# Constants packed on the host and loaded in few transfers, the attention's beside the filter's network, and that network on two chunks at once

## The chip, the core and the metric

The kernel runs on one core of one Trainium2 chip. A core has five engines that run side by side, each through its own instruction stream in order: TensorE (PE) for matmuls, VectorE (DVE), ScalarE (ACT), GpSimd (POOL) and SyncE (SP). In this kernel SP issues all transfers between DRAM and the on-chip memory; the transfers themselves are done by 16 DMA engines. The metric is the device time of one run, in microseconds (us), taken as the median of several runs. The time before is 12442.48 us, the median of 3 runs from 12437.2 to 12442.61.

## What is computed

The input x is [32, 192, 56, 56] in f32. Four layers follow each other, each with a group normalisation in front (32 groups) and a residual sum:

```python
x = x + _L0_conv_ref(_gn(x), ...)   # agent attention: qkv, 49 pooled agents, 6 heads, 3x3 depthwise, projection
x = x + _L1_conv_ref(_gn(x), ...)   # two-way WKV scan over 3136 tokens, layer norm, output projection
x = x + _L2_conv_ref(_gn(x), ...)   # shift by rounded offsets, then a 3x3 Gaussian of the remainder
x = x + _L3_conv_ref(_gn(x), ...)   # long convolution with a generated 55x55 filter, by FFT
```

The filter of the last layer comes from a small network over the 55 x 55 = 3025 positions:

```python
h = jnp.sin(f1 * (jnp.einsum('bchw,oc->bohw', z, W1) + b1))     # 32 -> 64
h = jnp.sin(f2 * (jnp.einsum('bchw,oc->bohw', h, W2) + b2))     # 64 -> 64
k = jnp.einsum('bchw,oc->bohw', h, W3)                          # 64 -> 192
k = k * (jnp.exp(-distance_map * jnp.abs(deltas)) + shift)
```

Its Fourier spectrum doesn't depend on the images and is needed only in the last layer.

## The kernel before

`all_blocks` (L1813) calls four parts one after the other: `make_filter` (L201), `attention` (L321), `scan_pairs` (L898, with a guarded second version that is entered only if a count is above zero) and `channel_blocks` (L1509). Between the parts the images go through DRAM (`x1`, `x2`). The parts are written in a framework in which each engine's order comes from a scheduler, and waits are put in where a tile's data or its memory demand it. A part's tiles come from pools that are opened in the part; the pools of the next part take over the same memory, and what is written there first waits for what used it last.

**The filter.** SP loads 12 constants (helper L212, issued at L214). The network (loop of 11 chunks of 275 positions, before `loaded`) does for each chunk: matmul with W1 (L261), a sine (`sine`, L243), matmul with W2 (L264), a second sine, a copy into `h2_i` (L267). A sine is seven DVE instructions (L246 to L253: scale, range reduction, clamp) and one of ACT (L255). W1's and W2's outputs are 64 rows, so these instructions work on 64 of 128 partitions. Chunk i's second sine and chunk i+1's first run interleaved. Then for each half t of the 192 channels the decay (ACT, L275) and, chunk by chunk, the product with W3 (PE, L278) times decay (DVE, L280); half t is stored to `filt` (SP, L285). The products of t = 0 are spread over the network's loop by the scheduler; those of t = 1 follow it. The second stage reads `filt` back in six batches of 32 channels (L301), makes spectra by two matmuls each with copies on ACT and DVE (L1801, L1807, L311, L314) and stores them to `spectra`.

**The attention.** Before its first image SP issues 128 transfers for constants: weights of q, k and v in forms for 128 and 64 or 65 rows (L348), the projection's blocks (`_Pairs.blocks`, L860 to L864), vectors (L870, L872), matrices for norms and heads (L348), four pieces of an interpolation matrix into rows 64 to 124 of `xs_c` (61 rows each, L397), and two tables of bias coefficients, `gk_c` and `gq_c`, in 96 small transfers (L407 to L410). Then images 0 and 1 are loaded (`load`, L445). For an image: statistics (`moments`, L452: L457 and L459 BatchNorm statistics, L461/L462, row sums L466, pooled sums L469 to L477), group sums on PE (L487), scale and offset (L504 to L509), pooled agents (L520), keys of the agents (L532, L533, `seen`), normalised image pieces `xs_a` and `xs_c` (L544, L548), values (`find_v`, L563 to L576), depthwise taps (L589, L591), and then the loop over images that begins with `weigh` (L596; matmuls L604, L605). Inside the loop the next image is loaded and its statistics are taken beside the current one's matmuls.

**The scan's start.** 52 constant transfers: two halves each of Wo, the layer norm's gain and bias and a centring matrix, 24 blocks and more for Wk, Wv, Wr, the output matrix, centring, mean and group (`blocks`), and two vectors in three pieces each. The output matrix `wog` is Wo times the gain, centred; it is made by L941 to L951, written to DRAM (`wogT`, L952) and read back in six blocks. Behind them SP loads the sums of squares (`seen`, L1053) that the attention has left in DRAM; from these come group means on PE (L1016 and on), and the first normalisation is ACT's L1100. The decay and bonus vectors pass through L963 to L980 first.

**The channel blocks' start.** Nine constants (L1530), eight whole memsets of `padded` on POOL (L1539), then the offsets (`off`, L1544) and a chain of small DVE instructions (L1545 to L1572) that makes the taps' weights; POOL makes the shift matrices (L1586 to L1591) and PE starts with L1594.

Of the kernel before, what the change touches and what calls it, by code (L numbers as in the profile page):

```python
# [29 lines left out]
T = 96  # L30
# [44 lines left out]

def _constants():
# [16 lines left out]
    for t in range(2):  # L93
# [4 lines left out]
    heads = np.kron(np.eye(2), np.ones((AG, HD)))  # L98
    return {
        "spread": spread,  # L100
        "norm4": norm4.reshape(128, 4, 128),
        "ident": np.eye(128),
        "group": group,
        "center": center,
        "group192": np.kron(np.eye(C // GROUP), np.ones((GROUP, GROUP))) / GROUP,
        "centre": np.eye(C) - 1.0 / C,
        "mean192": np.full((C, C), 1.0 / C),
        "mean": np.full((T, T), 1.0 / C),
        "heads": heads,
        **_spectral_constants(),  # L110
# [90 lines left out]
def make_filter(ctx: ExitStack, tc: tile.TileContext, a, consts, filt, spectra):  # L201
# [3 lines left out]
    wp = ctx.enter_context(tc.tile_pool(name="f_w", bufs=2))  # L205
    pp = ctx.enter_context(tc.tile_pool(name="f_p", bufs=2, space=PSUM))
# [5 lines left out]
    def load(name, shape, ap):  # L212
# [5 lines left out]
    w2 = load("w2", [FO, FO], a["L3_conv_W2T"])  # L218
    w3 = load("w3", [FO, C], a["L3_conv_W3T"])
    z = load("z", [FE, P2], a["L3_conv_z"].rearrange("b c h w -> (b c) (h w)"))  # L220
    bs = [load(k, [FO, 1], a[f"L3_conv_{k}"].unsqueeze(1)) for k in ("b1", "b2")]
    fs = [
        load(k, [FO, 1], a[f"L3_conv_{k}"].rearrange("a c h w -> c (a h w)"))
        for k in ("f1", "f2")
    ]
    per = {}
    for k in ("deltas", "shift", "bias"):
        per[k] = load(
            k, [T, 2], a[f"L3_conv_{k}"].rearrange("a (t p) h w -> p (a t h w)", p=T)
        )  # L230
    dist = load(
        "dist", [T, P2], a["L3_conv_distance_map"].rearrange("a b h w -> (a b h w)").partition_broadcast(T)
    )
    nd = cp.tile([T, 2], F32, name="nd", tag="nd")
# [8 lines left out]
    def sine(ps, b, f):  # L243

        v = wp.tile([FO, n], F32, name="v", tag="v")
        nc.vector.tensor_scalar(v, ps, b, f, ALU.add, ALU.mult)  # L246
        m = wp.tile([FO, n], F32, name="m", tag="m")
        nc.vector.tensor_scalar(m, v, 1.0 / (2.0 * math.pi), None, ALU.mult)
        nc.vector.tensor_scalar(m, m, BIG, None, ALU.add)
        nc.vector.tensor_scalar(m, m, BIG, None, ALU.subtract)  # L250
        nc.vector.scalar_tensor_tensor(v, m, -C1, v, ALU.mult, ALU.add)
        nc.vector.scalar_tensor_tensor(v, m, -C2, v, ALU.mult, ALU.add)
        nc.vector.tensor_scalar(v, v, EDGE, -EDGE, ALU.min, ALU.max)  # L253
        h = wp.tile([FO, n], F32, name="h", tag="h")
        last = nc.scalar.activation(h, v, AF.Sin)  # L255
        return h, last

    sines = []
    for i in range(KS // RC):
        p1 = pp.tile([FO, BANK], F32, name="p1", tag="p1")  # L260
        nc.tensor.matmul(p1[:, :n], w1, z[:, i * n : (i + 1) * n], start=True, stop=True)  # L261
        h1, _ = sine(p1[:, :n], bs[0], fs[0])
        p2 = pp.tile([FO, BANK], F32, name="p2", tag="p1")
        nc.tensor.matmul(p2[:, :n], w2, h1, start=True, stop=True)  # L264
        h2, last = sine(p2[:, :n], bs[1], fs[1])
        keep = cp.tile([FO, n], F32, name=f"h2_{i}", tag=f"h2_{i}")
        nc.vector.tensor_copy(keep, h2)  # L267
        sines.append(keep)
# [4 lines left out]
    for t in range(2):  # L273
        decay = wp.tile([T, P2], F32, name="decay", tag="decay")
        nc.scalar.activation(decay, dist, AF.Exp, scale=nd[:, t : t + 1])  # L275
        for i in range(KS // RC):
            p3 = pp.tile([T, BANK], F32, name="p3", tag="p3")
            nc.tensor.matmul(p3[:, :n], w3[:, t * T : (t + 1) * T], sines[i], start=True, stop=True)  # L278
# [40 lines left out]

@with_exitstack  # L320
def attention(ctx: ExitStack, tc: tile.TileContext, a, k, x1, st_a, st_c):  # L321
# [11 lines left out]
    xp = ctx.enter_context(tc.tile_pool(name="a_x", bufs=2))  # L333
# [11 lines left out]
    def const(name, shape, *parts):  # L345
        t = cp.tile(shape, F32, name=name, tag=name)
        for to, ap in parts:
            nc.sync.dma_start(out=to(t), in_=ap)  # L348
        return t

    def all_of(t):
        return t

    pairs = _Pairs(nc, cp)
    qkv, qkvb = a["L0_conv_Wqkv"], a["L0_conv_bqkv"]

    def taking(name, col):

        return (
            const(f"{name}_a", [128, C], (all_of, qkv[0:128, col : col + C])),  # L360
            const(
                f"{name}_c",
                [65, C],
                (lambda t: t[0:64], qkv[128:C, col : col + C]),
                (lambda t: t[64:65], qkvb[col : col + C].unsqueeze(0)),
            ),
        )

    def giving(name, row):

        w = a["L0_conv_WqkvT"]
        return (
            const(f"{name}_a", [128, C + 1], (all_of, w[row : row + 128])),
            const(f"{name}_c", [64, C + 1], (all_of, w[row + 128 : row + C])),
        )

    wq, wv = taking("wq", 0), taking("wv", 2 * C)
    wqT, wkT = giving("wqT", 0), giving("wkT", C)
    proj = pairs.blocks("proj", a["L0_conv_proj_w"])
    pb, dwb = pairs.vector("pb", a["L0_conv_proj_b"]), pairs.vector("dwb", a["L0_conv_dwc_b"])  # L380
    dw = a["L0_conv_dwc_w"].rearrange("p o h w -> p (o h w)")
    dww = const(
        "dww",
        [128, 2, 9],
        (lambda t: t[:, 0, :], dw[0:128]),
        (lambda t: t[UP, 1, :], dw[128:C]),
        (lambda t: t[LOW, 1, :], dw[128:C]),
    )
    ident = const("ident", [128, 128], (all_of, k["ident"]))
    norm4 = const("norm4", [128, 4, 128], (all_of, k["norm4"]))  # L390
    heads = const("heads", [PAIR, 2 * HD], (all_of, k["heads"]))
# [3 lines left out]
    xs_c = [cp.tile([128, S * w], F32, name=f"xs_c{j}", tag=f"xs_c{j}") for j, w in enumerate(WIDTHS)]  # L395
    for j, w in enumerate(WIDTHS):
        nc.sync.dma_start(out=xs_c[j][64:KC], in_=k["spread"][:, S * STARTS[j] : S * (STARTS[j] + w)])  # L397

    def coefficients(name, grid, cols, rows):

        t = cp.tile([128, 2 * NK, HA], F32, name=name, tag=name)
        nc.gpsimd.memset(t, 0.0)
        g = grid.rearrange("(y x) c -> y x c", x=POOL)
        for j, w in enumerate(WIDTHS):
            for h in range(2):
                y0, x0 = 3 * h, GRID[j]
                nc.sync.dma_start(out=t[65:93, 2 * j + h], in_=rows[28 * h : 28 * h + 28])  # L407
                nc.sync.dma_start(out=t[93 : 93 + w, 2 * j + h], in_=cols[STARTS[j] : STARTS[j] + w])
                for y in range(4):
                    nc.sync.dma_start(out=t[109 + 4 * y : 113 + 4 * y, 2 * j + h], in_=g[y0 + y, x0 : x0 + 4])  # L410
        return t

    gk_c = coefficients("gk_c", a["anT"], a["awT"], a["ahT"])
    gq_c = coefficients("gq_c", a["naT"], a["waT"], a["haT"])
# [29 lines left out]

    def load(b):  # L445
        x = xp.tile([128, S, S], F32, name="x_a", tag="x_a"), xp.tile([128, S // 2, S], F32, name="x_c", tag="x_c")
        nc.sync.dma_start(out=x[0], in_=a["x"][b, 0:128])
        for h, r in HALVES:
            nc.sync.dma_start(out=x[1][r], in_=a["x"][b, 128:C, 28 * h : 28 * h + 28])
        return x  # L450
# [318 lines left out]
    nxt = load(0)  # L769
# [8 lines left out]
    for b in range(NB):  # L778
        x, more = nxt, b + 1 < NB
        if more:  # L780
            nxt = load(b + 1)
# [58 lines left out]
class _Pairs:  # L840
# [3 lines left out]
    def __init__(self, nc, pool):  # L844
        self.nc, self.pool = nc, pool

    def blocks(self, name, ap, inner=True):

        nc = self.nc
        aa = self.pool.tile([128, 128], F32, name=f"{name}_aa", tag=f"{name}_aa")  # L850
        ca = self.pool.tile([128, 128], F32, name=f"{name}_ca", tag=f"{name}_ca")
        if not inner:
            nc.sync.dma_start(out=aa, in_=ap[0:128, 0:128])
            for r in (slice(0, 64), slice(64, 128)):
                nc.sync.dma_start(out=ca[r], in_=ap[128:C, 0:128])
            return aa, ca, None, None
        ac = self.pool.tile([128, 64], F32, name=f"{name}_ac", tag=f"{name}_ac")
        cc = self.pool.tile([128, 128], F32, name=f"{name}_cc", tag=f"{name}_cc")
        nc.gpsimd.memset(cc, 0.0)  # L859
        nc.sync.dma_start(out=aa, in_=ap[0:128, 0:128])  # L860
        nc.sync.dma_start(out=ac, in_=ap[0:128, 128:C])
        for r in (slice(0, 64), slice(64, 128)):
            nc.sync.dma_start(out=ca[r], in_=ap[128:C, 0:128])
            nc.sync.dma_start(out=cc[r, r], in_=ap[128:C, 128:C])  # L864
        return aa, ca, ac, cc

    def vector(self, name, ap):

        t = self.pool.tile([128, 2], F32, name=name, tag=name)
        self.nc.sync.dma_start(out=t[:, 0:1], in_=ap[0:128].unsqueeze(1))  # L870
        for r in (slice(0, 64), slice(64, 128)):
# [1009 lines left out]
```

## Time and profile before

| | |
|---|---|
| median of 3 runs | 12442.48 us |
| profiled execution, its own time | 12448.77 us |
| span of that execution | 12447.0 us |
| mean granted TensorE clock | 0.96 |
| instructions | 164748 |
| moved by DMA | 719.51 MB, mean 58 GB/s |
| filter | 0 to 178 us |
| attention: set-up and first image, then its loop | 178 to 312, then to 5012 us |
| scan: start, then its loop | 5012 to 5068, then to 8521 us |
| channel blocks: start, then their loop | 8521 to 8540, then to 12447 us |

All times below are from the profiled execution, counted from the start of its span. The page lists for each engine the busy time, its share of the span and the number of instructions; under that, 40 slices with one digit per slice, where 9 means busy 90% or more. PEclk is the granted clock of TensorE in tenths. PEld is the load of weights, which overlaps with PE. In a timeline a row begins with the start and the duration; in brackets at its end is the idle time of that engine before it, and what ended it. SPq rows are issues of transfers: their duration is that of issuing, not of the transfer.

### The profile page before, as it was taken

The numbers are of one execution on the slowest core, as the hardware profiler recorded it, in microseconds if no ns is written. First come the engines' busy times: TensorE is split into PE (matmuls) and PEld (weight loads), VectorE is DVE, ScalarE is ACT, GpSimd is POOL, SyncE is SP. The second block draws the span as 40 slices with busy tenths as digits, with TensorE's granted clock in tenths as the row PEclk, the third lists the DMA queues.
The fourth block names the chain that finished last, engine by engine and source line by source line (L and its number), as shares of the span: only waits on it lengthen the run. The fifth ranks groups of instructions, "written<-read, shape, count | busy, mean of one in ns | idle before, by whom it ended". The sixth has DMA issues, their size and how long they took to land. (4 is left out here: it accounts for less than half of the span.)

```text
span 12447.0 us, 164748 instructions
## 1 busy us (share of the span) xinstructions
PE 11356.6 (91%) x62738; PEld 7114.0 (57%) x62738; DVE 10861.2 (87%) x15560; ACT 6217.0 (50%) x11820; POOL 2303.7 (19%) x2237
## 2 busy tenths in 40 slices
PE   4999999999999999788888888888999999999999
PEld 1555555555555655333333333335777777777777
DVE  3888888888888888799999999997888888888888
ACT  2555555555555555466666666663333333333333
POOL 0000000000000000465555565552000000000000
PEclk7999999999999999899999999998999999999999
DMA  2111111111111111233444343432111111111111
GB/s 65 32 50 40 40 40 40 40 40 42 54 43 40 40 40 32 73 98 96 102 102 100 95 98 97 102 98 77 42 44 42 42 44 42 45 42 43 42 43 29
DMA packets 940870, 719.51 MB, mean 58 GB/s; under 512 B 777295, under 2 KB 818746, under 8 KB 931057
## 3 DMA queue, kind: packets, MB, share of 16 engines
q1 hardware_dynamic: 929832, 683.18, 21.3%
q10 hardware_dynamic: 10240, 25.70, 0.8%
q8 instruction: 500, 8.19, 0.3%
q14 instruction: 298, 2.43, 0.1%
HBM read 403.11 MB, written 240.80 MB: 52 GB/s over the span
## 5 line engine op out<-in xcount | busy, mean ns | idle before, releaser
L591 DVE SCALAR_TENSOR_TENSOR o<-v_a,dww,o 128x896 f32<-128x896 f32 (+1 forms) x1024 | 1056.9, 1032 | 408.1 <-ACT v_a L565 291.8
L1807 ACT COPY y<-ps 64x252 f32<-64x252 f32 (+1 forms) x2376 | 809.6, 341 | 1134.3 <-PE ps L1801 1104.0
L1725 PE MATMUL ps<-f,real 84*84 84x112 f32 x6144 | 1090.8, 259 | 0.0
L1725 PE MATMUL ps<-f,imag 84*84 84x112 f32 x6144 | 1089.4, 259 | 0.0
L1732 ACT COPY z<-ps 84x448 f32<-84x448 f32 x768 | 406.2, 529 | 1217.1 <-PE ps L1725 1215.6
L859 POOL MEMSET Wk_cc<- 128x128 f32 x1 | 0.2, 205 | 4819.7 <-DVE x_c L757 4819.7
L1725 PEld LDWEIGHTS ps<-f,real 84*84 84x84 f32 x6144 | 783.9, 153 | 134.2 <-issue 95.8
L1725 PEld LDWEIGHTS ps<-f,imag 84*84 84x84 f32 x6144 | 763.8, 153 | 0.0
L1125 ACT ACTIVATE q<-q 128x784 f32<-128x784 f32 x384 | 328.7, 856 | 808.9 <-DVE q L1120 637.8
L881 PE MATMUL ps<-sq,mean_aa 128*128 128x392 f32 x512 | 301.7, 753 | 424.6 <-ACT sq L1203 424.6
L591 DVE SCALAR_TENSOR_TENSOR o<-v_c,dww,o 128x448 f32<-128x448 f32 (+1 forms) x1024 | 638.5, 623 | 5.2
L604 PE MATMUL ps<-xs_a,gk_a 128*98 128x448 f32 (+1 forms) x1536 | 639.6, 497 | 0.0
L605 PE MATMUL ps<-xs_c,gk_c 125*98 125x448 f32 (+1 forms) x1536 | 633.1, 493 | 0.0
L608 ACT ACTIVATE pr<-ps,low 98x896 f32<-98x896 f32 (+1 forms) x384 | 352.3, 918 | 557.1 <-DVE low L606 557.1
L1591 POOL TENSOR_TENSOR mat<-tap,tap 114x114 f32<-114x114 f32 x96 | 40.8, 425 | 3166.6 <-PE ps L1651 2313.1
L696 PE MATMUL ps<-gq_a,xs_a 128*112 128x294 f32 x1792 | 603.3, 418 | 19.0 <-DVE pq L701 19.0
L1742 PE MATMUL ps<-z,f 84*114 84x448 f32 x1536 | 608.9, 539 | 0.0
L697 PE MATMUL ps<-gq_c,xs_c 125*112 125x294 f32 x1792 | 595.1, 413 | 0.0
L1699 PE MATMUL re<-y,f 128*84 128x420 f32 (+1 forms) x1152 | 532.2, 542 | 8.8 <-ACT y L1807 7.7
L1801 PEld LDWEIGHTS ps<-f,padded 114*128 114x128 f32 x3168 | 473.3, 192 | 96.7 <-issue 70.3
L1699 PE MATMUL im<-y,f 128*84 128x420 f32 (+1 forms) x1152 | 526.9, 538 | 0.0
L1801 PE MATMUL ps<-f,padded 114*128 114x168 f32 x3168 | 503.7, 310 | 21.6 <-DVE o L1744 10.2
(397 smaller groups left out, 29260.2 us busy)
## 6 DMA issues: line engine op xcount, KB each, us to landing
x<-x SPq DMA_DIRECT2D x512, 392.0 KB
x<-x SPq DMA_DIRECT2D x512, 196.0 KB
x<-x SPq DMA_DIRECT2D x192, 399.0 KB
out_x<-x SPq DMA_DIRECT2D x384, 196.0 KB
x_a<-in_x SPq DMA_DIRECT2D x32, 1568.0 KB
x<-x_a SPq DMA_DIRECT2D x32, 1568.0 KB
x_c<-in_x SPq DMA_DIRECT2D x64, 392.0 KB
x<-x_c SPq DMA_DIRECT2D x64, 392.0 KB
```

What stands on the lines that cost most here:

```text
L591: nc.vector.scalar_tensor_tensor(dst, tap(i), dww[:, t, i : i + 1], dst, ALU.mult, ALU.add)
L604: mm(ps[P2, h, :n], g[:, cols], xs_a[j][:, px], start=True, stop=False)
L605: mm(ps[P2, h, :n], gk_c[0:KC, 2 * j + h, cols], xs_c[j][0:KC, px], start=False, stop=True)
L608: nc.scalar.activation(pr[:, :, :n], ps[P2, :, :n], AF.Exp, bias=low[:, j, p : p + 1], accum_out=sums[:, j, p : p + 1])
L696: mm(ps[:SUB, i, :HA], xs_a[j][:, px], g, start=True, stop=False)
L697: mm(ps[:SUB, i, :HA], xs_c[j][0:KC, px], gq_c[0:KC, 2 * j + (q + i) // ns], start=False, stop=True)
L1699: nc.tensor.matmul(ps[:, : n * 84], f2[:, i, :], y[:, i0 : i0 + n].rearrange("p g s u -> p (g s u)"), start=True, stop=True)
L1725: nc.tensor.matmul(ps[:84, i * 2 * S : (i + 1) * 2 * S], part[:, i0 + i].rearrange("p s u -> p (s u)"), f3[:, m, :], start=(m == 0), stop= ...
L1732: nc.scalar.copy(z[:, i0 : i0 + n].rearrange("p g m w -> p (g m w)"), ps[:84, : n * 2 * S])
L1742: nc.tensor.matmul(got, f4[:, m, :], z[:, i0 : i0 + n, m, :], start=(m == 0), stop=(m == 1))
L1801: nc.tensor.matmul(ps[:, g * 168 : (g + 1) * 168], flat[:, (g0 + g) * 128 : (g0 + g + 1) * 128], f1, start=True, stop=True)
L1807: nc.scalar.copy(y[64 * m : 64 * m + 64, 2 * g0 + i : 2 * (g0 + n) : 2], got[64 * i : 64 * i + 64, :, :, m, :])
```

## The change

On the host: constants are laid out in arrays that go straight into tiles. `att_k` (128 x 704) holds identity, norm and head matrices; `att_w` (128 x 1240) and `att_c` (65 x 770) the attention's weights; `coef_k` and `coef_q` (60 x 8 x 294) the coefficient tables with their zeros; `scan_o`, `scan_c`, `scan_w` (128 x 1348) and `scan_k` (128 x 1152) the scan's; `chan_k` (128 x 1244) the channel blocks' nine; `filter_w` (128 x 324) and `filter_p` the filter's, with W2 twice on a diagonal of 128 x 128 and W3 and the vectors twice above each other.

In the kernel: the filter loads five arrays instead of 12, and right behind them issues image 0 and all constants of the attention, into pools that stay open over both parts. Its network works on pairs of chunks in partitions 0 to 63 and 64 to 127; there are 6 pairs, the last with chunk 10 in both halves. The decay has one buffer instead of two. The scan's start has four constant transfers, and `wog` is made in on-chip memory. The channel blocks load the offsets first and all else in one transfer, and clear only columns 56 to 63 of `padded`. The memsets of the coefficient tables and of the blocks are gone. In the order of the compiled change, the loads of image 1 follow on SP behind those constants, ahead of the stores to `filt`; the BatchNorm statistics of images 0 and 1 stand among the network's instructions on DVE, image 1's ahead of the network's last sine; the row sums L466 wait for the last store of spectra. The loops over images are unchanged.

```diff
-def make_filter(ctx: ExitStack, tc: tile.TileContext, a, consts, filt, spectra):
+def make_filter(ctx: ExitStack, tc: tile.TileContext, a, consts, filt, spectra, beside):
...
+    dp = ctx.enter_context(tc.tile_pool(name="f_d", bufs=1))
...
-    w2 = load("w2", [FO, FO], a["L3_conv_W2T"])
-    w3 = load("w3", [FO, C], a["L3_conv_W3T"])
     z = load("z", [FE, P2], a["L3_conv_z"].rearrange("b c h w -> (b c) (h w)"))
...
+    ws = load("ws", [128, 128 + C + 4], a["filter_w"])
+    w2, w3 = ws[:, 0:128], ws[:, 128 : 128 + C]
+    b1, f_1, b2, f_2 = (ws[:, 128 + C + i : 129 + C + i] for i in range(4))
+    ends = load("ends", [T, 3, 2], a["filter_p"])
...
     dist = load(
         "dist", [T, P2], a["L3_conv_distance_map"].rearrange("a b h w -> (a b h w)").partition_broadcast(T)
     )
+    beside()
...
-        v = wp.tile([FO, n], F32, name="v", tag="v")
+        v = wp.tile([128, n], F32, name="v", tag="v")
...
-    for i in range(KS // RC):
-        p1 = pp.tile([FO, BANK], F32, name="p1", tag="p1")
-        nc.tensor.matmul(p1[:, :n], w1, z[:, i * n : (i + 1) * n], start=True, stop=True)
-        h1, _ = sine(p1[:, :n], bs[0], fs[0])
+    for i in range(0, KS // RC, 2):
+        p1 = pp.tile([128, BANK], F32, name="p1", tag="p1")
+        for h in range(2):
+            c = min(i + h, KS // RC - 1)
+            nc.tensor.matmul(p1[FO * h : FO * h + FO, :n], w1, z[:, c * n : (c + 1) * n], start=True, stop=True)
+        h1, _ = sine(p1[:, :n], b1, f_1)
...
-        decay = wp.tile([T, P2], F32, name="decay", tag="decay")
+        decay = dp.tile([T, P2], F32, name="decay", tag="decay")
...
+class _Ready:
...
+    def image(self, nc, a, b):
+        x = [self.images.tile([128, n, S], F32, name=f"x_{n}", tag=f"x_{n}") for n in (S, S // 2)]
+        nc.sync.dma_start(out=x[0], in_=a["x"][b, 0:128])
+        for h, r in ((0, slice(0, 64)), (1, slice(64, 128))):
+            nc.sync.dma_start(out=x[1][r], in_=a["x"][b, 128:C, 28 * h : 28 * h + 28])
+        return x
+
+    def load(self, nc, a, k):
+        self.first = self.image(nc, a, 0)
+        for to, ap in ((self.k, k["att_k"]), (self.w, a["att_w"]), (self.c, a["att_c"])):
+            nc.sync.dma_start(out=to, in_=ap)
+        for to, ap in ((self.gk_c, a["coef_k"]), (self.gq_c, a["coef_q"])):
+            nc.sync.dma_start(out=to[65:KC], in_=ap)
+        for j, w in enumerate(WIDTHS):
+            nc.sync.dma_start(out=self.xs_c[j][64:KC], in_=k["spread"][:, S * STARTS[j] : S * (STARTS[j] + w)])
...
-    nxt = load(0)
+    nxt = ready.first
...
+    weights, fixed = small("weights", [128, 1348]), small("fixed", [128, 1152])
+    nc.sync.dma_start(out=weights, in_=a["scan_w"])
+    nc.sync.dma_start(out=fixed, in_=k["scan_k"])
...
-        nc.sync.dma_start(out=wogT[r], in_=turn)
...
+    nc.vector.memset(wogs[:, 320:448], 0.0)
+    nc.vector.tensor_copy(wog[0], ps[:, 0, 0:128])
+    nc.vector.tensor_copy(wog[2], ps[:, 0, 128:C])
+    nc.vector.tensor_copy(wog[1], ps[:, 1, 0:128])
+    for r in (slice(0, 64), slice(64, 128)):
+        nc.vector.tensor_copy(wog[3][r, r], ps[r, 1, 128:C])
...
+    nc.sync.dma_start(out=off, in_=a["L2_conv_offset"].partition_broadcast(PR))
+    fixed = cp.tile([128, k["chan_k"].shape[1]], F32, name="fixed", tag="fixed")
+    nc.sync.dma_start(out=fixed, in_=k["chan_k"])
...
-        nc.gpsimd.memset(t, 0.0)
+        nc.gpsimd.memset(t[:, :, S:64], 0.0)
...
+    with tc.tile_pool(name="a_r", bufs=1) as rp, tc.tile_pool(name="a_x", bufs=2) as xp:
+        ready = _Ready(rp, xp)
+        make_filter(tc, a, k, filt, spectra, lambda: ready.load(nc, a, k))
+        attention(tc, a, ready, x1, st_a, st_c)
```

## The prediction

> **What bounds the kernel now.** I read the page first: busy rows, then slices.
>
> ```profile
> PE 11356.6 (91%) x62738; PEld 7114.0 (57%) x62738; DVE 10861.2 (87%) x15560; ACT 6217.0 (50%) x11820; POOL 2303.7 (19%) x2237
> ...
> PE   4999999999999999788888888888999999999999
> ...
> PEclk7999999999999999899999999998999999999999
> ```
>
> One digit is 311 us. PE is full everywhere except the first slice and where the blocks meet (the scan, 5012 to 8521, is held by DVE). None of the long loops is touched: attention (312 to 5012), scan and channel blocks keep their matmuls and transfers, and in the order in which the compiled change puts instructions on the engines they stand as before. So the time can only come from the first slice and the joints. I cut those out, in windows (busy time and count of PE, PEld, DVE, ACT, POOL, then granted clock, DMA share, GB/s):
>
> ```profile
> 0.00:178.00 178.00, 99.58 (x256) 40.27 (x256) 85.37 (x228) 47.16 (x102) 2.03 (x6) 0.98 0.25 67
> 178.00:265.00 87.00, 0.00 (x0) 0.00 (x0) 0.36 (x1) 0.00 (x0) 9.19 (x9) 0.50 0.22 60
> 265.00:312.00 47.00, 32.16 (x72) 15.28 (x73) 26.52 (x49) 20.76 (x37) 0.00 (x0) 0.51 0.24 70
> 312.00:5012.00 4700.00, 4508.18 (x25722) 2777.75 (x25720) 4051.84 (x6133) 2578.96 (x4603) 0.94 (x6) 0.98 0.14 41
> 5012.00:5068.00 56.00, 15.99 (x54) 11.49 (x55) 8.36 (x49) 6.01 (x11) 1.46 (x29) 0.50 0.38 101
> ...
> 8521.00:8540.00 19.00, 0.72 (x2) 0.46 (x2) 4.77 (x22) 0.44 (x1) 13.21 (x18) 0.50 0.37 114
> ```
>
> In 178 to 265 no engine computes; 47 us of first image follow at half clock, then 56 and 19 us at the other joints. The waits of the first 330 us (engine, line, releaser: total, times, longest) say what is missing:
>
> ```profile
> POOL proj_cc L859 <- DMA spectra<-g: 176.1, 1, 176.1
> ...
> DVE st_a L457 <- DMA x_a<-in_x: 91.3, 1, 91.3
> ```
>
> The attention's set-up starts only when the filter's last store has landed, and image 0 is queued on SP behind 128 constant transfers.
>
> **The filter's network.** Twelve stretches of two interleaved sines serve 11 chunks: in the timeline L246 starts one at 7.84, 12.39, 21.46 and 30.09 and then every 7.39, the last sine ends at 92.57, and the second `filt` store is issued at 104.80:
>
> ```profile
> 89.20 0.56 DVE L246 TENSOR_SCALAR v<-p,b,f 64x275 f32<-64x275 f32 x1 [0.61 <-PE p L264]
> ...
> 92.57 0.30 DVE L267 COPY h<-h 64x275 f32<-64x275 f32 x1 [0.56 <-ACT h L255]
> ...
> 104.80 0.30 SPq L285 DMA_DIRECT2D filt<-out  x1
> ```
>
> Six pairs make seven stretches, so five of 7.39 go: -36.95. A DVE or ACT instruction on 128 partitions is taken at the price of one on 64, since 275 elements a partition stay. The two 64-column matmuls of a pair go to different column halves; nearest row is L570, four such matmuls in 1.76 us against 1.86 for two of L563 with 128 columns, so a pair costs about 1.2, not 2.2. The start is 1.04 earlier: `z` is issued second instead of fourth (it was waited for until 6.66). Each stretch now carries two products L280 (0.50) for one: +0.42 in five, 2.1. The scheduler also puts image 0's statistics into the network (7 x 0.54 + 4 x 0.49 = 5.8 us of DVE); DVE idles 2.2 us a stretch, so I charge 1.4. The decay tile has one buffer instead of two: its second exponential (2.82, at 20.33 before, hidden) waits for the last first-half product and stands on the path, +2.9 (0 to 4). Together -31.6 without the next item.
>
> **The queue.** SP now gets image 0, att_k, att_w, att_c, the coefficients, four `xs_c` pieces and then image 1, all ahead of the filt stores. In before the four pieces look like this:
>
> ```profile
> 193.94 15.55 SPq L397 DMA_DIRECT2D xs_c<-in_spread  x4
> 209.58 2.95 SPq L407 DMA_DIRECT2D gk_c<-in_ahT  x1
> 212.58 5.60 SPq L408 DMA_DIRECT2D gk_c<-in_awT  x1
> ```
>
> and the window 198 to 214 has
>
> ```profile
> 198.00:214.00 16.00, 0.00 (x0) 0.00 (x0) 0.00 (x0) 0.00 (x0) 0.00 (x0) 0.50 0.07 28
> ```
>
> 0.07 is about one engine in sixteen; the packets run from 196.3 to 226.4, 30 us for 747 KB. The Trainium skill ("DMA: Bandwidth & Descriptors", section "Why a DMA increments its semaphore by 16 and not by 1") says that a transfer is spread over the largest number up to 16 that divides the row count: 61 rows, one engine. By size alone, at the 314 GB/s that images 0 and 1 reached (4.7 MB in 15 us from 259), the pieces would take 2.4 us and image 1 would be there at about 33. By the row they hold one engine from some 24 to 54.5, and the sixteenth of image 1 that this engine carries lands at about 61. This speaks against the change, because DVE reaches image 1's first statistics (L457, in order ahead of the last stretch) at about 49: it stops for 12 us (0 to 20), and ACT and PE behind it. I take the row. So the second filt store goes out at 104.80 - 31.6 + 12 = 85.2; that is -19.6.
>
> **From the spectra to the attention's loop.** The 68.6 us from that store to the last copy L314 (173.37) are unchanged: six batches of 9.68 bound by PE, DVE and the copies; end at 153.8. Before, 133.7 us lay between this copy and the first weigh matmul (L604 at 307.11): landing of the spectra, 79 us of constants (178.47 to 257.42), 7.2 for image 0, then 42.5 of work. After, constants and image are there. What still waits for the landing (4.97) is what takes over the filter's memory: the row sums L466. Then DVE has 3.41 + 1.73 + 0.84 + 0.98 and small ones, and image 1's sums (3.4), which the order puts ahead: 11.0; from the pooled agents (L520 at 282.51) to L604 24.6 as before, less 0.3 that now overlap. 40.3 in all, so L604 comes at 194.1. **The start saves 113 us**: 19.6 in the filter and 93.4 behind it.
>
> Here a second rule is weighed. These 24 us hold matmuls without a gap from 288.20:
>
> ```profile
> 300.00:306.00 6.00, 6.00 (x12) 2.12 (x12) 0.00 (x0) 1.76 (x2) 0.00 (x0) 0.50 0.00 0
> 306.00:312.00 6.00, 6.00 (x12) 2.13 (x9) 0.00 (x0) 4.29 (x7) 0.00 (x0) 0.56 0.00 1
> 312.00:320.00 8.00, 8.00 (x27) 3.68 (x26) 7.54 (x9) 1.79 (x4) 0.00 (x0) 1.00 0.01 3
> ```
>
> The granted clock stayed 0.50 for 23 us. "TensorE: Matmul & The Clock Gate", Part 1, has it full after some 3.4 us of sustained work: L604 would come about 8 us sooner still, saving 121. I take the trace, since the same matmuls follow a pause of PE again (16 us here), and keep 8 for the range.
>
> **Scan start.** 52 transfers (5013.55 to 5048.0, about 0.65 each) and a round trip of `wog` through DRAM become four transfers; six memsets go, which POOL did unseen. Set by:
>
> ```profile
> 5048.58 0.20 ACT L963 ACTIVATE w<-wd 128x2 f32<-128x2 f32 x1 [40.45 <-DMA wd<-in_L_conv_w_decay]
> ```
>
> From there 14.5 us lead to the first normalisation (L1100, 5063.08). After: four issues from 5013.6 behind the last image's stores, weights landing about 5021, the means' and groups' matrix 5023, `seen` 5024.5; the new `wog` matmuls and copies (3.6 for the matmuls of L949, five copies of about 0.3) sit in the in-order PE and DVE ahead of `part` until about 5027; the `near` chain (about 3.5) overlaps partly; `part` at 5030.5 and 9.7 to L1100 as before: 5040. **-23** (15 to 30; SP's image loads, issued from 5050.35 on before and needed at 5063, come forward by as much).
>
> **Channel start.** `off` is issued first instead of behind nine constants:
>
> ```profile
> 8526.16 0.33 SPq L1544 DMA_DIRECT2D off<-in_L_conv_offset  x1
> ...
> 8528.87 0.21 DVE L1545 TENSOR_SCALAR off<-off 114x96 f32<-114x96 f32 x1 [6.95 <-DMA off<-in_L_conv_offset]
> ```
>
> The chain to the first taps (L1586, 8534.00) moves by 4.07. Its next need is the packed matrix, 637 KB, at 8527, about when L1564 asks; the POOL memsets (8 x 0.95) shrink and would otherwise end at the same 8529. **-4** (0 to 5).
>
> **Sum** 113 + 23 + 4 = 140. Profiled: span 12447.0, execution 12448.77, which is 6.3 above the median of 12442.48; I state it against the median: 12302.
>
> **Rivals.**
> A. The start is worth less: image 1 later (a stall of 20 and more), the row sums waiting on more than I see, or the second decay worse; 25 us less: 12327. For it: four pieces on one engine, and an in-order DVE. Against: the landing is worked out from the same pieces.
> B. No stall, or the clock comes up quickly: 12 or 8 us more, or both: 12282 to 12294, 12288 in the middle. For it: at the scan start the clock rose 5 us after 5064. Against: the 23 us above.
> C. Slower, one mechanism: the loop of 32 images (147 us each) runs PE near 96% at a clock of 0.98; if the new places of tiles and the earlier loads of x make each image wait 4.4 us, the 140 are gone; at 5.3 us an image it gives 12472. For it: images come through the same SP queue. Against: PE is the bound there, DMA share 0.14.
> D. The constants aren't early after all, because SP stands in the issue of the pieces (15.55 us for four) or memory isn't free: only the filter, scan and part of the joint gain, about 50: 12392. Against: the filt stores come 25 us and more after the last piece is issued, and the tiles have memory of their own.
>
> **How the numbers follow.** Forecast 0.53 (its own range 12293 to 12314), A 0.22, B 0.16, D 0.04, C 0.05. The range 12272 to 12335 takes in A and B but for their tails, and the ends of all bounds except the joint worst. About 0.2% (25 us) is what a measurement of this kernel can tell from no change: faster 0.95 (forecast, A, B, D), same 0.02 and slower 0.03 (both of C).
>
> **What would show it.** Right: the second filt store near 85, a DVE wait of some 12 us for x_a inside the network, the first weigh matmul near 194, the normalisation at the scan 23 us sooner counted from the last image's store, loops of equal length (4700, 3453, 3907). Wrong: no pause in the network (B), DVE waiting for DMA after 160 (A), or a longer loop (C).

## The result and the profile after

The changed kernel takes 12294.84 us (median of 4 runs, 12291.28 to 12299.31) against 12442.55 before (4 runs, 12437.2 to 12446.93): a ratio of 0.988, 95% interval 0.9865 to 0.9895, or 147.7 us less. The forecast was 12302. The page of the changed kernel:

```profile
PE 11329.2 (92%) x62734; PEld 7107.7 (58%) x62734; DVE 10836.4 (88%) x15489; ACT 6205.0 (50%) x11808; POOL 2250.7 (18%) x2228
...
PE   7999999999999999788888888888999999999999
...
PEclk9999999999999999999999999999999999999999
```

Nearly all that changed sits in the first digit of the PE row, 4 to 7. The stages are told by the same kind of windows as before:

```profile
0.00:157.00 157.00, 87.80 (x248) 38.56 (x248) 71.83 (x179) 40.33 (x90) 2.23 (x7) 0.99 0.45 121
157.00:190.00 33.00, 18.47 (x65) 9.66 (x65) 18.40 (x27) 18.06 (x32) 4.84 (x6) 0.69 0.17 46
190.00:4882.00 4692.00, 4507.19 (x25730) 2779.72 (x25728) 4049.67 (x6132) 2579.88 (x4609) 0.00 (x0) 0.98 0.14 41
4882.00:4911.00 29.00, 13.77 (x52) 9.86 (x52) 8.05 (x52) 1.62 (x6) 1.46 (x29) 0.50 0.71 193
4911.00:8371.00 3460.00, 2860.27 (x10434) 1303.98 (x10434) 3318.65 (x3431) 2180.36 (x3744) 1923.90 (x1699) 0.92 0.39 97
8371.00:8387.00 16.00, 0.73 (x2) 0.46 (x2) 5.22 (x23) 0.44 (x1) 7.54 (x18) 0.50 0.39 130
8387.00:12292.00 3905.00, 3841.00 (x26206) 2965.42 (x26206) 3364.61 (x5648) 1384.30 (x3328) 310.73 (x471) 1.00 0.17 42
```

The window without compute (178 to 265 before) is gone, the filter is 21 us shorter, the three loops have kept their work. Cut at instructions that both kernels have (the stores of an image are the SP issues that write `x1`), with a second profile of the kernel before (first experiment) beside the first:

| stretch (us) | before, 1st | before, 2nd | after | forecast of the difference |
|---|---|---|---|---|
| start to the store of image 0 | 468.0 | 457.7 | 342.0 | -113 |
| from there to the last image's store | 4542.7 | 4537.6 | 4539.6 | 0 |
| to the scan's first normalisation | 52.3 | 52.3 | 28.8 | -23 |
| scan loop | 3458.0 | 3456.6 | 3460.2 | 0 |
| channel blocks' start | 18.2 | 18.3 | 15.4 | -4 |
| channel loop | 3907.7 | 3907.6 | 3906.8 | 0 |
| sum (to the last instruction) | 12447.0 | 12430.0 | 12292.8 | -140 |

The two profiles of one kernel lie 17 us apart, 10 of it in the first row and 5 in the second. So single stretches are read to some 5 us, and the first to 10; against the two profiles the change is worth 154 and 137 us, with the medians' 148 between them.

Where the filter now waits is seen in the timeline of the changed kernel (start, duration, queue or engine):

```profile
15.23 24.83 SPq L361 DMA_DIRECT2D xs_c<-in_spread  x4
...
40.10 9.87 SPq L226 DMA_DIRECT2D f<-in_f  x2
...
50.01 0.51 SPq L349 DMA_DIRECT2D x<-in_x  x1
...
64.22 0.63 DVE L438 BATCH_NORM_STATS2 st_a<-x 128x6 f32<-128x448 f32 x1 [17.27 <-DMA x<-in_x]
...
87.00 0.31 SPq L294 DMA_DIRECT2D filt<-out  x1
```

SP stands 25 us in the issue of the four one-engine pieces and 10 in that of `f`; only then, at 50.0, does image 1 go out. DVE, in order, has stood 17.3 us at its statistics, in the middle of the network. Between 32 and 40 the DMA share is 0.06, about one engine of sixteen. That is the wait that the prediction named, at 12 us.

### The profile page after: what moved, and what is told of

Read it like the earlier page. It is cut to its first block, busy times and chain, and to the rows that moved or that the text cites. A ratio compares the mean times of both kernels' runs of the same rounds, so it can differ in the third digit from the quotient of the medians.

```text
span 12292.8 us, 164375 instructions
## 1 busy us (share of the span) xinstructions
PE 11329.2 (92%) x62734; PEld 7107.7 (58%) x62734; DVE 10836.4 (88%) x15489; ACT 6205.0 (50%) x11808; POOL 2250.7 (18%) x2228
## 3 DMA queue, kind: packets, MB, share of 16 engines
q1 hardware_dynamic: 919020, 683.39, 21.7%
## 5 line engine op out<-in xcount | busy, mean ns | idle before, releaser
L572 DVE SCALAR_TENSOR_TENSOR o<-v_a,att_w,o 128x896 f32<-128x896 f32 (+1 forms) x1024 | 1053.8, 1029 | 418.6 <-ACT v_a L546 291.5
L1681 PE MATMUL ps<-fixed,real 84*84 84x112 f32 x6144 | 1090.9, 259 | 0.0
L1681 PE MATMUL ps<-fixed,imag 84*84 84x112 f32 x6144 | 1089.5, 259 | 0.0
L1681 PEld LDWEIGHTS ps<-fixed,real 84*84 84x84 f32 x6144 | 784.0, 153 | 134.2 <-issue 95.8
L1681 PEld LDWEIGHTS ps<-fixed,imag 84*84 84x84 f32 x6144 | 763.8, 153 | 0.0
L572 DVE SCALAR_TENSOR_TENSOR o<-v_c,att_w,o 128x448 f32<-128x448 f32 (+1 forms) x1024 | 635.0, 620 | 5.1
L677 PE MATMUL ps<-gq_a,xs_a 128*112 128x294 f32 x1792 | 602.8, 417 | 19.2 <-DVE pq L682 19.2
L1698 PE MATMUL ps<-z,fixed 84*114 84x448 f32 x1536 | 608.8, 539 | 0.0
L834 PE MATMUL ps<-x,weights 128*128 128x392 f32 x1536 | 577.4, 519 | 27.5 <-DVE bv L1108 14.2
L1655 PE MATMUL re<-y,fixed 128*84 128x420 f32 (+1 forms) x1152 | 532.3, 543 | 8.7 <-ACT y L1763 7.6
L1655 PE MATMUL im<-y,fixed 128*84 128x420 f32 (+1 forms) x1152 | 526.9, 538 | 0.0
```

Source lines behind the costliest of these rows:

```text
L572: nc.vector.scalar_tensor_tensor(dst, tap(i), dww[:, t, i : i + 1], dst, ALU.mult, ALU.add)
L677: mm(ps[:SUB, i, :HA], xs_a[j][:, px], g, start=True, stop=False)
L834: mm(out, aa, srcs[t][h], start=True, stop=False)
L1655: nc.tensor.matmul(ps[:, : n * 84], f2[:, i, :], y[:, i0 : i0 + n].rearrange("p g s u -> p (g s u)"), start=True, stop=True)
L1681: nc.tensor.matmul(ps[:84, i * 2 * S : (i + 1) * 2 * S], part[:, i0 + i].rearrange("p s u -> p (s u)"), f3[:, m, :], start=(m == 0), stop= ...
L1698: nc.tensor.matmul(got, f4[:, m, :], z[:, i0 : i0 + n, m, :], start=(m == 0), stop=(m == 1))
```

## The experiments

Ten runs follow; the first and the tenth repeat the two kernels, with one execution each. Where a time is given it is the median of 4 executions, unless it is called a span (of the profiled one). Beside them the kernel before was measured again, with medians of 12439.16 (experiments 1 to 4), 12435.97 (5 to 8) and 12437.71 (9 and 10) against 12442.55 above. So a difference of less than some 7 us between medians of different groups is not read. In the code, "..." marks what is left out.

**1. The kernel before once more**, without an edit.

> The kernel before, unchanged, once more, for its stages and its granted clock. In the first profile the matmuls of image 0 ran without a gap from 288.2 and the clock stayed at half until 311.3; in the changed kernel it rose at 182.1, 3.6 us after they became dense at 178.5. Theory 1: the 101 us in which PE stood still before them makes the clock rise late; then this profile again shows about 20 us or more between the dense matmuls and the rise. Theory 2: it was chance of one execution; then it rises within 3 to 8 us this time, and the first weigh matmul comes at about 299 instead of 307. The long loops should differ from the first profile by no more than 5 us each; what they differ by is the bound for reading stage lengths.

Measured: one run of 12431.83, span 12430.0. The same two windows from the first profile of the kernel before, then from this one:

```profile
288.50:292.50 4.00, 4.00 (x6) 1.86 (x6) 3.99 (x5) 3.94 (x7) 0.00 (x0) 0.50 0.33 79
292.50:296.00 3.50, 3.50 (x7) 0.86 (x7) 0.50 (x4) 3.47 (x6) 0.00 (x0) 0.50 0.34 85
```

```profile
288.50:292.50 4.00, 4.00 (x7) 1.93 (x7) 3.99 (x5) 3.82 (x6) 0.00 (x0) 0.50 0.27 62
292.50:296.00 3.50, 3.50 (x14) 1.26 (x13) 0.84 (x4) 3.46 (x7) 0.00 (x0) 0.96 0.42 104
```

Matmuls without a gap in both, but here the clock is up after 4.3 us and 14 matmuls fit where 7 did; the first weigh matmul comes at 300.4 instead of 307.1. The pause of PE ahead of them is as long (101.3 and 102.0 us), so its length isn't the cause. The 23 us on which I had built were one execution's.

**2. Pieces of 64 rows.**

```diff
-        "spread": spread,
+        "spread": np.pad(spread, ((0, 3), (0, 0))),
...
-            nc.sync.dma_start(out=self.xs_c[j][64:KC], in_=k["spread"][:, S * STARTS[j] : S * (STARTS[j] + w)])
+            nc.sync.dma_start(out=self.xs_c[j][64:128], in_=k["spread"][:, S * STARTS[j] : S * (STARTS[j] + w)])
```

> The changed kernel with one edit: the interpolation pieces are padded from 61 to 64 rows, so that each can go over 16 DMA engines instead of one. Theory 1 (one engine carries the pieces, image 1 queues behind them, and DVE in its order waits 17.3 us for image 1 inside the filter's network): the pieces take 3 us instead of 31, image 1 lands before 45, the wait at image 1's statistics falls under 2 us, the second filt store moves from 87.0 to 70 (68 to 72), the span falls by 17 us to about 12276. Theory 2 (the wait comes from the bytes in the queue or from SP's issuing, not from the row count): pieces and wait stay as they are, store at 87, span within 3 us of 12293.

Measured: 12278.1 (12271.18 to 12280.41), span 12275.9, ratio to before 0.987 (0.9854 to 0.9887). Its timeline:

```profile
15.90 4.78 SPq L361 DMA_DIRECT2D xs_c<-in_spread  x4
...
25.53 0.35 SPq L349 DMA_DIRECT2D x<-in_x  x1
...
70.20 0.30 SPq L294 DMA_DIRECT2D filt<-out  x1
```

Three rows of zeros more, and the pieces are issued in 4.8 us instead of 24.8, image 1 goes out at 25.5, DVE no longer waits for it, and the second store comes at 70.2. The wait is due to the row count: the edit adds bytes, and only the number of rows is better. This agrees with the rule of the Trainium skill ("DMA: Bandwidth & Descriptors", section "Why a DMA increments its semaphore by 16 and not by 1") that was weighed: 61 has no divisor up to 16 but 1, 64 has 16.

**3. Two decay buffers.**

```diff
-    dp = ctx.enter_context(tc.tile_pool(name="f_d", bufs=1))
+    dp = ctx.enter_context(tc.tile_pool(name="f_d", bufs=2))
```

> The changed kernel with one edit: the decay tile has two buffers again, pieces as in the change (61 rows). In the compiled order this also puts the statistics of images 0 and 1 behind the network's last product on DVE, ahead of the spectra's copies. Theory 1: both the second exponential (2.9 us on the path) and the wait of 17.3 us for image 1 leave the network's path; the second filt store comes at 65 (63 to 68) instead of 87.0; the statistics (10 us) are covered, because DVE's first spectra copy comes 14.9 us after the last product; span about 12271 (-22). Theory 2: the statistics behind the products wait for image 1 until 64 and then hold up the spectra's copies: the store at 65, but the last spectra copy no more than 8 us earlier than in the change (157.3), span about 12285.

Measured: 12274.9 (12270.47 to 12281.66), ratio 0.9868 (0.9851 to 0.9884). From its timeline:

```profile
58.38 10.33 SPq L294 DMA_DIRECT2D filt<-out  x2
...
68.40 3.78 DVE L438 BATCH_NORM_STATS2 st_a<-x 128x6 f32<-128x448 f32 x7
...
74.58 3.78 DVE L438 BATCH_NORM_STATS2 st_a<-x 128x6 f32<-128x448 f32 x7
...
138.20 0.68 DVE L323 COPY g<-ps 84x504 f32<-84x504 f32 x1 [0.17 <-PE ps L320]
```

The second store is at 68.4, just past the window that was expected, and the last spectra copy ends at 138.9 instead of 157.3, so theory 2 falls: the statistics now stand behind the products, none of them waits, and they are covered. The span of the profile was 12279.9, 9 over the expected 12271. The second store came 3 late, and from the first dense matmul to its store the first image took 9 more than in the changed kernel: the clock took 13.2 us to rise and not 3.6, and later was at half for 17.1 us instead of 10.2. What followed was 4 shorter. The buffer matters less for its 2.9 us than for the order. That the order changes with it is seen; the reason, that with one buffer memory was free beside the filter and the scheduler used it for the statistics, is my reading and not shown.

**4. One chunk at a time**, on 64 partitions, with all else as changed.

```diff
-    for i in range(0, KS // RC, 2):
+    for i in range(KS // RC):
...
-        v = wp.tile([128, n], F32, name="v", tag="v")
+        v = wp.tile([FO, n], F32, name="v", tag="v")
```

> The changed kernel with the network on one chunk at a time, as before (12 stretches on 64 partitions), everything else as changed. Theory 1 (two chunks save 31.6 us of network, of which the wait for image 1 eats most): without two chunks image 1 is there before it is asked for, the second filt store comes at 107 (104 to 109), that is 20 us later than the changed kernel's 87.0, and the span is about 12313. Theory 2 (the two chunks bring their 32 to 37 us whatever image 1 does): store at 119 to 124, span about 12327. If two chunks bring nothing, the store is at 87.

Measured: 12310.13 (12304.12 to 12315.45), 15 over the changed kernel, span 12313.7. There is no wait for image 1, and the second store is issued at 103.3, just below the expected 104 to 109:

```profile
103.31 0.30 SPq L291 DMA_DIRECT2D filt<-out  x1
```

This is nearest to theory 1: of the 33 us that two chunks save once image 1 is out of the way (103.3 against 70.2 in the second experiment), the changed kernel sees 16 at the store. The store came 3.7 earlier than expected: with one buffer one of two early exponentials, with its table loads, leaves the network's start, which I had charged at its end but not credited there. In the kernel before, the stretches from 12.39 and 21.46 took 9.1 and 8.6 us; here, without the second exponential, they take 7.4.

**5. Loads behind the filter.** Packed constants and image 0 wait until the filter has left its memory.

```diff
-    with tc.tile_pool(name="a_r", bufs=1) as rp, tc.tile_pool(name="a_x", bufs=2) as xp:
-        ready = _Ready(rp, xp)
-        make_filter(tc, a, k, filt, spectra, lambda: ready.load(nc, a, k))
+    make_filter(tc, a, k, filt, spectra, lambda: None)
+    with tc.tile_pool(name="a_r", bufs=1) as rp, tc.tile_pool(name="a_x", bufs=2) as xp:
+        ready = _Ready(rp, xp)
+        ready.load(nc, a, k)
```

> The changed kernel with the attention's packed constants and image 0 loaded after the filter, into memory that the filter has left, instead of beside its network. What is tested is how much of the 117 us that the start lost lies in the packing (128 transfers to 7, and four pieces) and how much in loading early. Theory 1 (packing carries most): the network has no wait for image 1 and its second filt store comes at 71 (69 to 74); after the last spectra copy (about 141) image 0 lands near 155, and image 1 near 198 because it queues behind the one-engine pieces; DVE waits for it ahead of the depthwise taps, which start at about 206 instead of 188; span 12311 (12300 to 12322), that is 18 us over the changed kernel. Theory 2 (early loading carries it): image 0 and the constants cost the joint 45 us or more; span 12338 or over.

Measured: 12312.71 (12307.06 to 12317.61), 18 over the changed kernel, as theory 1 had it; counted from the kernel before beside each, it is 24. In its timeline the wait has only moved:

```profile
200.59 3.78 DVE L438 BATCH_NORM_STATS2 st_a<-x 128x6 f32<-128x448 f32 x7 [29.88 <-DMA x<-in_x]
...
207.61 1.14 DVE L572 SCALAR_TENSOR_TENSOR o<-v_a,att_w,o 128x896 f32<-128x896 f32 x1
```

DVE waits 29.9 us for image 1 behind the pieces, and the taps start at 207.6 against 188.0. In the network that wait is gone (second store 67.4, under the expected 69 to 74). So loading early brings some 18 to 24 us net, and the two chunks 15 in the fourth experiment. Most of the 148 us is left for the packing, by subtraction; no run has the packing alone.

**6. The output matrix behind the means** (the block from L893 to L911 of the changed kernel moved behind `nb1`).

> The changed kernel with one edit: at the scan's start the output matrix (its matmuls, gain and five copies) is made after the group means instead of ahead of them. Theory 1 (my prediction's step: on in-order PE and DVE that work stands ahead of the means; in the changed kernel DVE waits 3.9 us for L905 and the means' first reduction L1011 comes at 4899.5): the time from the last image's store to the first normalisation falls from 28.8 to about 21 (19 to 24), span by 7 us. Theory 2 (the constants' landing sets it): no more than 2 us.

Measured: 12295.28 (12289.78 to 12301.49), nothing. The stretch fell from 28.8 to 27.3. Its timeline says why:

```profile
4902.22 0.20 ACT L895 ACTIVATE eu<-weights 128x2 f32<-128x2 f32 x1 [13.45 <-DMA weights<-in_scan_w]
...
4906.16 0.42 DVE L993 TENSOR_REDUCE part<-seen 128x64 f32<-128x256 f32 x1
...
4917.93 0.16 DVE L1017 COPY cb<-ps 128x2 f32<-128x2 f32 x1 [1.95 <-PE ps L1016]
```

The last store was issued at 4891.4; the weights land 10.8 later, the decay's chain then stands ahead of the means on DVE, and the moved block gets in again ahead of `nb1` (2.2 us). The first normalisation then comes at 4918.7. Theory 1 falls: without the output matrix ahead of them, the landing and this chain hold the means nearly as long.

**7. Row sums in memory of their own**, with two decay buffers; the lines that make the new tiles are left out here.

```diff
-        by_x = [wp.tile([128, n, POOL], F32, name="by_x", tag=f"by_x{n}", bufs=1) for n in (S, S // 2)]
+        by_x = ready.by_x
```

> The kernel with two decay buffers and a second edit: the row sums have memory of their own beside the filter, so that they need not wait for the last store of spectra. In its order they stand between the network's last product and the first spectra copies. Theory 1 (the landing of 5 us and 11 us of DVE's row sums are on the path between the last spectra copy and the dense matmuls of image 0, which took 21.2 us in the changed kernel and the same with two decay buffers): that stretch falls to about 10.5 (9 to 13), while the first spectra copies come up to 4 us later; span 6 us below the 12280 of the two-buffer run, 12270 to 12276 in the median's terms about 12268. Theory 2 (something else, such as the memory of the normalised pieces, holds the matmuls): the stretch stays over 18.

Measured: 12272.08 (12268.9 to 12275.53), span 12273.7. The last spectra copy and the first dense matmul of image 0, from the changed kernel's timeline and from this one:

```profile
156.65 0.68 DVE L323 COPY g<-ps 84x504 f32<-84x504 f32 x1 [0.23 <-PE ps L320]
...
178.52 1.86 PE L544 MATMUL ps<-xs_a,att_w 128*128 128x448 f32 x2
```


```profile
142.32 0.68 DVE L323 COPY g<-ps 84x504 f32<-84x504 f32 x1 [0.17 <-PE ps L320]
...
153.63 1.86 PE L545 MATMUL ps<-xs_a,att_w 128*128 128x448 f32 x2
```

It is 10.6 us from the end of the one to the other, where it was 21.2, in the third experiment too; the last copy came 4.1 later than there. That row sums, pushed behind the spectra's landing, stood on the path is shown. The gain of 6 in the span is there; in the medians it is 3, which these runs can't tell from nothing. The edit has a side effect: DVE again waits for the first maximum of image 0 ahead of the depthwise taps (23.4 us), as in the kernel before and not in the changed one (see "The taps" below).

**8. All four edits.**

> The changed kernel with four edits together: pieces of 64 rows, two decay buffers, row sums in memory of their own, output matrix after the means. If the parts add up (about 22 for the first two, which cover the same wait, 6 for the third, 7 for the fourth), the time is 12295 - 35 = 12260 (12248 to 12270). If the granted clock's rise or the spectra copies eat the third, 12266.

Measured: 12270.16 (12266.39 to 12278.33), span 12267.9, ratio to before 0.9868 (0.9851 to 0.9884). The gain in the span is 25 us (25 in the medians, or 18 if each is counted from the kernel before beside it), and the parts don't add to 35. The profiles show where the 10 are lost: the scan's start is 26.5 instead of 28.8 us, 2 of the 7 that were expected, and from the first weigh matmul to the store of image 0 it is 157.5 us instead of the changed kernel's 152.0: DVE waits for the first maximum ahead of the taps here too (19.2 us), and the clock is at half for 13.7 us of it instead of 10.2. It is the fastest median here, but those of the second, third, seventh and ninth lie within its range.

**9. Sums of squares first.** On top of those, the scan's start loads `fixed` and `seen` ahead of the weights, takes the means ahead of the decay's chain, and makes the output matrix after the first piece.

> The kernel with the four edits, and the scan's start re-ordered: the group matrix and the sums of squares are loaded first and the weights behind them, the means come before the decay's chain, and the output matrix is made after the first piece of the first pair. Theory 1 (in the run with the output matrix late, the weights' landing 10.8 us after the last store and then 3.6 us of the decay's chain on DVE stood ahead of the means, and 2.2 us of the output matrix ahead of the first normalisation): the stretch from the last image's store to the first normalisation falls from 26.5 to 20.5 (19 to 23). Theory 2 (whatever is issued first lands only when the last image's stores have left the queues, so the order of the loads doesn't matter, and only the chain's 3.6 us go): 22.9 or more. The span falls by as much, to 12262 in a profile like that of the four edits (12267.9); a loss in the loop by the later output matrix would show as a longer scan loop than 3459.

Measured: 12272.43 (12266.69 to 12277.33), span 12264.8. The stretch is 20.3 us as expected, so the order of the loads and of DVE's work set it (they were changed together, so their shares stay open); the scan loop was 3462.0, 2.7 longer than with the four edits, which can't be told from the spread (3456.6 to 3461.8 in the other profiles). The median shows no gain, so this version isn't taken as better.

**10. The changed kernel once more.**

> The changed kernel once more, unchanged, for the spread of its stages. Nine profiles so far have the granted clock rise between 3.6 and 23 us after the matmuls of image 0 became dense. Theory 1 (it is chance of the execution, as between the two profiles of the kernel before): this profile differs from the first of the changed kernel (3.6 us), and the first image's store moves from 342.0 by about half of the difference in the rise. Theory 2 (each program has its own delay): 3 to 5 us again, and the store at 342 within 1.

Measured: one run of 12293.54, span 12291.7. The clock rose 4.1 us after the matmuls became dense, the store of image 0 came at 341.6: theory 2 as far as this program goes. But in the sixth experiment the engines go through the same instructions up to there, in the same order, and:

```profile
180.00:198.00 18.00, 18.00 (x32) 5.88 (x31) 6.39 (x8) 9.87 (x16) 0.00 (x0) 0.50 0.08 18
198.50:202.00 3.50, 3.50 (x10) 1.60 (x9) 3.50 (x6) 0.00 (x0) 0.00 (x0) 0.96 0.00 0
```

Its matmuls are dense from 175.8, the clock comes at 198.8. So a delay that belongs to the program doesn't explain it either. The two ran on different chips, but on the sixth's chip the fifth and eighth rose after 4.9 and 4.8 us, so the chip alone doesn't either.

## Why the prediction was right, point by point

**What bounds it.** Right: the loops moved by no more than 5 us, all the rest came from the first slice and the joints.

**The sum.** 140 us were forecast and 148 measured, which is closer than the terms are. The start was forecast at 113 and brought 126 against the first profile and 116 against the second. The first weigh matmul came at 190.0 instead of 194.1: 1.8 us late at the second store, 1.7 more up to the last spectra copy, then 0.5 and 7.1 early. Up to the store of image 0 another 5 to 9 us fell that no step had ("The taps"). The 7.1 and a part of these hang on a clock that differs from one execution to the next. That the sum was this close is in part luck.

**The network.** The second store was forecast at 85.2 and came at 87.0, from two errors that nearly cancel. The network itself was 3 us better than my -31.6 (70.2 in the second experiment, with the wait gone and the decay's wait still there), as much as the credit for the early exponential that I had left out. That 128 partitions cost what 64 do was right: L246 takes 0.56 us in both. The wait was 17.3 and not 12: image 1 landed at 64.2 instead of 61, and DVE asked for it at 46.9 instead of 49. I had let image 1 queue on the engine behind the pieces, but it wasn't even issued, because SP stood in the issue of the pieces and of `f` until 50.0. The cause, four one-engine pieces, and the sign were right; the path by which they delayed image 1 was only in part the one that I gave.

**From the spectra to the loop.** The stretch from the second store to the last spectra copy, which I had taken as unchanged, 68.6 us, took 70.3; no run shows why. 21.7 us were forecast from the last copy to the first dense matmul, 21.2 measured. The next term was mis-sized: I took 18.6 us from there to the first weigh matmul, with the clock at half as in the first profile; it took 11.5 (178.52 to 189.99). The part of rival B about the clock was true here. The first experiment shows that my row was a single draw.

**The taps.** In the changed order DVE takes the 16 taps of the first piece ahead of the first maximum (L587), instead of waiting 19.3 us for it and taking them after. I had read these orders as equal. The kernel before, then the changed one:

```profile
312.46 1.09 DVE L606 TENSOR_REDUCE low<-ps 98x1 f32<-98x896 f32 x1 [19.30 <-PE ps L605]
```

```profile
187.98 1.15 DVE L572 SCALAR_TENSOR_TENSOR o<-v_a,att_w,o 128x896 f32<-128x896 f32 x1 [10.86 <-ACT o L570]
...
201.25 3.08 DVE L587 TENSOR_REDUCE low<-ps 98x1 f32<-98x896 f32 x3
```

From the first weigh matmul to the store of image 0 it is 152.0 us, against 160.9 and 157.3 in the two profiles of the kernel before: 5 us or more that no step had. Not all of it is the order. With the taps ahead of the maximum this stretch took 151.7 to 156.6 us in six profiles (the fifth experiment, with its wait for image 1, left aside), with the taps behind 156.9 to 160.9 in five (the kernel before twice, experiments 7 to 9), and in both groups the clock was at half for 7 to 21 us of it. If half of that time is taken off, the groups are 147 to 148 and 150 to 152. So I estimate the order at some 3 us and put the rest down to the clock; no run changes the order alone.

**Scan start.** 23 forecast, 23.5 measured. What I named as last, the output matrix and then the means, is what the changed trace shows; from its waits (engine, line, releaser: total, times, longest):

```profile
PE ps L899 <- DMA passing<-in_scan_o: 11.1, 1, 11.1
...
DVE wogs L907 <- PE ps L905: 3.9, 1, 3.9
```

What would be late without it I had not worked out, and the sixth and ninth experiments show it to be the landing behind the last image's stores and the decay's chain.

**Channel start.** 4 forecast, 2.8 measured. The packed matrix lands after it is asked for:

```profile
8374.77 0.21 DVE L1501 TENSOR_SCALAR off<-off 114x96 f32<-114x96 f32 x1 [2.89 <-DMA off<-in_L_conv_offset]
...
8377.73 0.40 DVE L1520 TENSOR_SCALAR ok<-rnd,fixed 114x48 f32<-114x48 f32 x2 [0.58 <-DMA fixed<-in_chan_k]
...
8380.70 2.99 POOL L1542 TENSOR_SCALAR tap<-fixed,where,gs 114x114 f32<-114x114 f32 x4 [7.69 <-issue]
```

It is 5.93 us from the first instruction on the offsets to the first taps, where it was 5.13; most of the 0.8 is the 0.58 that DVE waits for the matrix. The offsets themselves came 3.6 sooner.

**Rivals.** A: its wait was 5 longer than taken, short of the 25 that it needed. B: half of it was true, the clock, and half false, since the wait in the network was there; by the time alone, 12294.84, it can't be told from the forecast, whose range it shares. C: no loop lost 4 us an image. D: the constants were early; the fifth experiment prices it at some 18 to 24 us rather than 90, because when they are late the wait for image 1 leaves the network.

## What to carry to other kernels

Constants are dear to fetch in a hundred pieces: 128 transfers held SP for 79 us here. Taking away the overlap cost some 18 to 24 us of the 148, so the packing seems to be most of the gain, though it was not measured alone. Before a transfer is moved ahead of others, look at how many rows it has: four pieces of 61 rows held up the network for 17 us, and three rows of padding freed it. An edit that moves work can also reorder what it doesn't touch, as the taps show. When an in-order engine gets early work whose data come late, that work stalls what stood behind it, so look in the compiled order at what lands next to what.

## What the hardware showed that was not expected

The delay from dense matmuls to the full clock was, over the twelve profiles at image 0, between 3.6 and 23.1 us, counted from the first matmul with `xs_a`: 3.6 and 4.1 in the two of the changed kernel, 23.1 and 4.3 in those of the kernel before, 23.0 in the sixth experiment, 13.1 to 13.6 in four others and 3.6 to 4.9 in the last three. PE was busy without a gap all the while. The Trainium skill ("TensorE: Matmul & The Clock Gate", Part 1) gives some 3.4 us of sustained activity. The short cases are near it, the long ones are not, and no run here settles what makes them long. From the first dense matmul to its store, image 0 took 9 us more in the sixth experiment than in the changed kernel, with the same instructions.

In the attention's loop three images in a row of the changed kernel, cut at their stores, read

```profile
342.00:488.00 146.00, 140.05 (x808) 86.64 (x807) 127.32 (x194) 81.25 (x146) 0.00 (x0) 0.99 0.15 42
488.00:637.00 149.00, 142.65 (x807) 86.94 (x806) 127.50 (x194) 81.10 (x145) 0.00 (x0) 0.97 0.15 41
637.00:783.40 146.40, 140.99 (x808) 87.08 (x807) 127.33 (x194) 81.23 (x146) 0.00 (x0) 0.98 0.15 42
```

The same work takes 146 to 149 us as the granted clock averages 0.99 to 0.97. The kernel before has the same three lengths at other images, and over the 31 images that follow the first the two differ by 3 us in the first profiles, less than the 5 by which the two profiles of the kernel before differ.
